# Taking the matrix values out of the gathers: an equality count on VectorE, and a scratch write among the row gathers

## The chip, the cores and the metric

The kernel runs on one core of one Trainium2 chip. A core has five engines that work side by side: PE (TensorE, matmul; its weight loads are listed apart as PEld), DVE (VectorE), ACT (ScalarE), POOL (GpSimd) and SP (SyncE, which here only issues transfers). Each takes its instructions in order and waits on semaphores for the others. The metric is the device time of one execution in microseconds, as the median of several runs without a profile.

## The reference, cut to what matters

Two graph layers run over one sparse matrix `adj` of 2708 x 2708 (about 1 % of it is not zero, and each row is divided by its number of entries, so all entries of a row are equal). Features are 128 wide.

```python
def layer0(X, A, W):                      # hyperbolic convolution
    XW = mobius_matvec(W, X)
    gamma = 2 / max(1 - sum(XW * XW), EPS)
    nominator   = A @ (gamma * XW)        # the dense product over adj
    denominator = clamp(A @ (gamma - 1))
    m = mobius_scalar_mul(0.5, nominator / denominator)
    return expmap0(relu(logmap0(mobius_scalar_mul(A.sum(-1), m))))

def layer1(x, A, msg_w, msg_b, upd_w, upd_b, ln_w, ln_b):
    s = x @ msg_w[:, :D].T
    d = x @ msg_w[:, D:].T
    messages   = gelu(s[:, None] + d[None, :] + msg_b)
    aggregated = einsum('ijd,ij->id', messages, A)      # only where A is not zero
    h = gelu(concat([x, aggregated]) @ upd_w.T + upd_b) + x
    return layernorm(h) * ln_w + ln_b

x = layernorm(x + layer0(x, adj, W))
x = layernorm(x + layer1(x, adj, ...))
```

## The kernel before

Rows are worked in 22 blocks of 128. While the dense product of layer 0 runs over a block of `adj`, the kernel also finds where the block is not zero: it takes signs, packs them into keys by matmul, reads the largest keys with `max`, and turns them into edges. The edges of a block are laid in tiles of 128, 99 tiles in all. For each tile it keeps `J` (the neighbour of each edge), `rid` (the edge's row within the block), `R` (a 0/1 matrix that carries rows to edges) and, before the change, `V` (the edge's value). GpSimd gathers V from the matrix in DRAM. Layer 1 then goes tile by tile: gather the neighbours' rows from a table, add, gelu, and sum by a matmul with `rv`.

```python
def gather(o, src, at):                                          # L189
    nc.gpsimd.indirect_dma_start(out=o, out_offset=None, in_=src,
        in_offset=bass.IndirectOffsetOnAxis(ap=at, axis=0))      # L191

def layer0(b):                                                   # one block
    aT = stream.tile([P, NB, P], F32, name="aT")                 # 2 buffers
    nc.sync.dma_start(aT, adj_t[b])                              # L317
    sgn = stream.tile([P, NB, P], BF16, name="sgn", bufs=1)
    nc.scalar.activation(sgn, aT, AF.Sign, accum_out=signs[:, b : b + 1])   # L319
    for j in range(NB):                                          # L324: the dense product
        if j in BREAKS: yield                                    # the steps of older blocks go in here
        nc.tensor.matmul(op[:, : D + 2], lhsT=aT[:, j, :], rhs=y[:, j, :], ...)
    nc.vector.scalar_tensor_tensor(nom[:, b, :], y[:, b, :], dg[:, b : b + 1], op, ...)   # L328
    ...                                                          # L332 ACT, L334 DVE: sums of squares

def keys(l, sgn):
    ...                                                          # L344, L350: keys by matmul into kp
    nc.vector.max(top[:, c : c + 8], seg[:, s, :])               # L358

def extract(l):
    ...                            # L378 to L389: lead, rest, second keys, m (in the list or not)
    nc.tensor.matmul(op[:, 0:2], lhsT=tri, rhs=db[:, 1:3], ...)  # L397, L398: running counts
    nc.scalar.copy(oe[:, l, :], op[:, 0:2])                      # L399
    nc.vector.scalar_tensor_tensor(mid, ...)                     # L402
    ...                            # L409 ACT, L412/L414 DVE: R from iota and mid
    yield
    ...                            # L419 to L429: bits, low, scan, code, z
    nc.tensor.matmul(sp[:, k, :], lhsT=R[:, t0 + k0 + k, :], rhs=z, ...)     # L438
    ...                            # L441, L446: nearest place; L444 rid
    nc.vector.scalar_tensor_tensor(J[:, t], near, -1.0, limit[:, t], ...)    # L447
    nc.vector.scalar_tensor_tensor(F[:, k0:k1], J[:, t], float(b * P * N - 1), rid[:, t], ...)  # L448
    for t in range(t0, t0 + n):
        gather(V[:, t : t + 1], adj.rearrange("i (j o) -> (i j) o", o=1), F[:, ...])

# between the layers
gd = nom
for g, n in quads:
    nc.scalar.activation(gd[:, g : g + n, :D], gd[:, g : g + n, :D], AF.Gelu)              # L583
    for k in range(n):
        nc.scalar.mul(gd[:, g + k, :D], gd[:, g + k, :D], dg[:, g + k : g + k + 1])        # L585

def messages(b, ag, tiles, ...):                                 # quads of up to four tiles
    for k, t in enumerate(ts):
        gather(dd[:, k, :], table..., J[:, t : t + 1])           # 7 quads of dd form a ring
        nc.tensor.matmul(X[:, k, :], lhsT=R[:, t, :], rhs=s_nm[:, b, :], ...)              # L652
        nc.vector.tensor_scalar(rv[:, k, :], iotaN, rid[:, t : t + 1], V[:, t : t + 1],
                                op0=OP.is_equal, op1=OP.mult)                              # L654
    nc.vector.tensor_tensor(dd, X, dd, op=OP.add)                # L657
    nc.scalar.activation(dd, dd, AF.Gelu)                        # L658
    for k in range(w):
        nc.tensor.matmul(ag[:, :P], lhsT=dd[:, k, :], rhs=rv[:, k, :], ...)                # L660

nc.scalar.copy(gd[:, b, :D], ag[:, :P])                          # L691, early blocks
nc.scalar.copy(agT, ag[:, :P])                                   # L702, all blocks
```

A dense fallback follows, taken only when a check on the lists fails; it does not run here.

## Time and profile before

| | |
|---|---|
| time, median of 3 runs | 389.42 us (389.2 to 390.23) |
| the profiled execution | 504.16 us, span 502.5 us, mean granted PE clock 0.783 |
| first product of layer 0 (L324) starts | 30.5 us into the span |
| last product of layer 0 starts | 268.3 us |
| first message sum (L660) starts | 344.6 us |
| last row gather starts | 451.75 us |
| GpSimd gathers of values | 99, median 944 ns each |
| GpSimd gathers of rows | 81 into `dd`, 18 into a free `aT` buffer, 944 ns each |
| transfers of `aT` | 22 of 1408 KB, median 6.7 us from issue to landing |

Times inside the span are those of one profiled execution, which is longer than the timed ones. In the lists of groups a line reads: source line, engine, operation, output and inputs with their sizes, count, then busy time, mean length in ns, and idle time of the engine before them with what ended it. In a timeline the first number is the start, the second the length. "remote" and "issue" mark waiting whose cause the trace does not show.

### The profile page before, as it was taken

The numbers are of one execution on the slowest core, as the hardware profiler recorded it, in microseconds if no ns is written. First come the engines' busy times: TensorE is split into PE (matmuls) and PEld (weight loads), VectorE is DVE, ScalarE is ACT, GpSimd is POOL, SyncE is SP. The second block draws the span as 40 slices with busy tenths as digits, with TensorE's granted clock in tenths as the row PEclk, the third lists the DMA queues.
The fourth block names the chain that finished last, engine by engine and source line by source line (L and its number), as shares of the span: only waits on it lengthen the run. The fifth ranks groups of instructions, "written<-read, shape, count | busy, mean of one in ns | idle before, by whom it ended". The sixth has DMA issues, their size and how long they took to land.

```text
span 502.5 us, 7784 instructions
## 1 busy us (share of the span) xinstructions
PE 333.5 (66%) x2427; PEld 297.2 (59%) x2427; DVE 275.9 (55%) x1474; ACT 208.0 (41%) x562; POOL 203.5 (40%) x297
## 2 busy tenths in 40 slices
PE   4269788674899989797973111538397697679620
PEld 4269677564889878795862001338395576557410
DVE  2979546433666565798740067248272226376671
ACT  2827325432657465794650022135032112326521
POOL 5301454571644525222257707722616572470000
PEclk9759779885999999998995555657679557798855
DMA  8306322223345544433421101110201120111100
GB/s 341 167 2 232 115 84 79 88 98 116 118 132 214 193 156 164 184 117 115 137 80 37 52 7 31 52 53 15 49 12 37 42 54 17 38 42 48 32 23 20
DMA packets 16237, 45.14 MB, mean 90 GB/s; under 512 B 5626, under 2 KB 11150, under 8 KB 13374
## 3 DMA queue, kind: packets, MB, share of 16 engines
q1 hardware_dynamic: 9710, 37.43, 20.6%
q0 software_dynamic: 6336, 6.55, 5.4%
q10 hardware_dynamic: 144, 0.60, 0.4%
q8 instruction: 20, 0.33, 0.3%
q14 instruction: 27, 0.22, 0.1%
HBM read 41.74 MB, written 2.83 MB: 89 GB/s over the span
## 4 chain that ended last, share of the span: by engine, by line
PE 32%; DVE 21%; issue 16%; another core or an unknown queue 14%; ACT 10%; DMA 4%; POOL 1%; DVEq 0%; POOLq 0%; ACTq 0%; SPq 0%
PE mp L324 7%; PE X L652 4%; PE mp L660 4%; PE kx L350 4%; PE sel L438 3%; DVE top L358 2%; ACT nom L635 2%; ACT sgn L319 2%; PE ag L660 2%; PE sel L612 1%; PE sel L613 1%; PE sel L610 1%; DMA xT<-in_x_t_dram 1%; DMA V<-in_adj_dram,F 1%
## 5 line engine op out<-in xcount | busy, mean ns | idle before, releaser
L191 POOL DMA_INDIRECT V<-in_adj_dram,F x99 | 94.9, 959 | 156.2 <-DVE top L358 31.0
L324 PE MATMUL mp<-y,aT 128*128 128x130 f32 x968 | 129.2, 288 | 1.4 <-DVE y L308 0.9
L324 PEld LDWEIGHTS mp<-y,aT 128*128 128x128 f32 x968 | 120.1, 199 | 2.3 <-DVE y L308 1.1
L191 POOL DMA_INDIRECT dd<-table_dram,J x81 | 78.1, 965 | 83.7 <-ACT agT L702 21.7
L319 ACT ACTIVATE sgn<-aT 128x2816 bf16<-128x2816 f32 x22 | 56.1, 2548 | 24.5 <-issue 20.5
L350 PE MATMUL kx<-kd,sgn 128*128 128x128 bf16 x484 | 41.5, 240 | 26.6 <-issue 19.1
L350 PEld LDWEIGHTS <-sgn 128*128 128x128 bf16 x484 | 33.3, 108 | 40.1 <-issue 31.4
L652 PE MATMUL X<-mx,R 128*128 128x128 f32 x198 | 41.1, 357 | 16.9 <-DVE dd L657 6.9
L654 DVE TENSOR_SCALAR rv<-iotaN,rid,V 128x128 f32<-128x128 f32 x99 | 30.1, 351 | 32.6 <-remote 20.0
L652 PEld LDWEIGHTS X<-mx,R 128*128 128x128 f32 x198 | 36.2, 265 | 19.2 <-DVE dd L657 7.5
L438 PE MATMUL sel<-z,R 128*128 128x49 f32 (+4 forms) x198 | 31.4, 299 | 23.3 <-DVE R L414 9.6
L438 PEld LDWEIGHTS sel<-z,R 128*128 128x128 f32 x198 | 28.3, 213 | 25.8 <-DVE R L414 10.4
L358 DVE MAX8 top<-kx 128x8 f32<-128x128 f32 (+3 forms) x152 | 28.6, 236 | 19.9 <-remote 14.8
L441 DVE TENSOR_TENSOR work<-sel,place 128x144 f32<-128x144 f32 (+11 forms) x29 | 11.7, 403 | 40.5 <-remote 30.9
L409 ACT ACTIVATE work<-iota,mid 128x512 f32<-128x512 f32 (+3 forms) x53 | 26.8, 553 | 5.5 <-DVE mid L402 5.4
L657 DVE TENSOR_TENSOR dd<-X,dd 128x384 f32<-128x384 f32 (+3 forms) x29 | 15.2, 526 | 21.7 <-remote 7.5
L444 ACT COPY rid<-sel 128x3 f32<-128x3 f32 (+5 forms) x29 | 4.7, 162 | 46.0 <-DVE work L441 36.3
L660 PE MATMUL mp<-rv,dd 128*128 128x128 f32 x116 | 21.6, 321 | 3.1 <-ACT dd L658 3.1
L402 DVE SCALAR_TENSOR_TENSOR mid<-sel,deg 128x2 f32<-128x2 f32 x25 | 3.9, 155 | 35.7 <-ACT oe L399 35.7
L610 PE MATMUL sel<-pk,xT 128*128 128x128 f32 x44 | 12.6, 377 | 16.4 <-ACT nom L614 10.4
L658 ACT ACTIVATE dd<-dd 128x384 f32<-128x384 f32 (+3 forms) x29 | 13.7, 497 | 20.3 <-DVE dd L657 14.5
L399 ACT COPY oe<-sel 128x2 f32<-128x2 f32 x25 | 4.0, 159 | 43.2 <-PE kx L350 25.9
(204 smaller groups left out, 614.6 us busy)
## 6 DMA issues: line engine op xcount, KB each, us to landing
aT<-in_adj_t_dram SPq DMA_DIRECT2D x22, 1408.0 KB, 6.7
V<-in_adj_dram,F POOLq DMA_INDIRECT x99
xT<-in_x_t_dram SPq DMA_DIRECT2D x2, 704.0 KB
x_sb<-in_x_nm_dram SPq DMA_DIRECT2D x2, 704.0 KB
out_dram<-nom SPq DMA_DIRECT2D x21, 64.0 KB, 1.6
dd<-table_dram,J POOLq DMA_INDIRECT x81
table_dram<-dt SPq DMA_DIRECT2D x5, 256.0 KB
pk<-in_pack_dram ACTq DMA_DIRECT2D x1, 587.5 KB
```

What stands on the lines that cost most here:

```text
L191: nc.gpsimd.indirect_dma_start(out=o, out_offset=None, in_=src, in_offset=bass.IndirectOffsetOnAxis(ap=at, axis=0))
L319: nc.scalar.activation(sgn, aT, AF.Sign, accum_out=signs[:, b : b + 1])
L324: nc.tensor.matmul(op[:, : D + 2], lhsT=aT[:, j, :], rhs=y[:, j, :], start=(j == 0), stop=(j == NB - 1))
L350: nc.tensor.matmul(kp[:, i * P : (i + 1) * P], lhsT=sgn[:, j, :], rhs=kd[:, q, :], start=False, stop=(i == len(groups) - 1 and j == j1 - 1),)
L358: nc.vector.max(top[:, c : c + 8], seg[:, s, :])
L409: nc.scalar.activation(r0, iota[:, k0 * P : k1 * P], AF.Abs, scale=2.0, bias=mid[:, k : k + 1])
L438: nc.tensor.matmul(sp[:, k, :], lhsT=R[:, t0 + k0 + k, :], rhs=z, start=True, stop=True)
L610: nc.tensor.matmul(up[:, :D], lhsT=x1T[:, s], rhs=wT[:, 2, :], start=True, stop=False)
L652: nc.tensor.matmul(X[:, k, :], lhsT=R[:, t, :], rhs=s_nm[:, b, :], start=True, stop=True)
L654: nc.vector.tensor_scalar(rv[:, k, :], iotaN, rid[:, t : t + 1], V[:, t : t + 1], op0=OP.is_equal, op1=OP.mult)
L657: nc.vector.tensor_tensor(dd, X, dd, op=OP.add)
L660: nc.tensor.matmul(ag[:, :P], lhsT=dd[:, k, :], rhs=rv[:, k, :], start=(first and k0 == 0 and k == 0), stop=(final and k0 + k == len(tiles ...
```

## The change

An edge's value is the same for the whole row of the matrix, and every row has its own diagonal element in it. So the value need not be fetched edge by edge: the sums can be made with ones, and multiplied at the end by the row's diagonal value. To be sure that this holds for the matrix at hand, VectorE compares every element of a block with the diagonal value of its row and counts the equal ones; the count is compared with the number of entries at the end, and the fallback is taken where they differ. So the gathers of V and the index F go; a 128 x 2816 comparison for each block comes, with a small load of the diagonal (`vb`); `rv` becomes a plain comparison for up to four tiles at once; the `dg` multiplications between the layers go; and the sum of a block is multiplied with a loaded row of diagonal values (`scaled`) where it was copied. Beside that the text has GpSimd write a scratch tile after each row gather, to keep two of them apart, and small column buffers are shared to make room.

```diff
@@ layer0
-    ss, ssp = cols(NB), cols(NB)
+    ss, ssp = (sc.tile([P, NB], F32, name=name) for name in ("ss", "ssp"))
     def layer0(b):
+        vb = stream.tile([P, P], F32, name="vb")
+        nc.sync.dma_start(vb, diag[:, b * P : (b + 1) * P].to_broadcast([P, P]))
         aT = stream.tile([P, NB, P], F32, name="aT")
         nc.sync.dma_start(aT, adj_t[b])
         sgn = stream.tile([P, NB, P], BF16, name="sgn", bufs=1)
         nc.scalar.activation(sgn, aT, AF.Sign, accum_out=signs[:, b : b + 1])
+        eq = stream.tile([P, NB, P], mybir.dt.uint8, name="eq", bufs=1)
+        nc.vector.scalar_tensor_tensor(
+            eq, aT, 1.0, vb.unsqueeze(1).to_broadcast([P, NB, P]),
+            op0=OP.mult, op1=OP.is_equal, accum_out=same[:, b : b + 1],
+        )
@@ extract
-        F = small.tile([P, TMAX], U32, name="F", bufs=3)
...
-            nc.vector.scalar_tensor_tensor(
-                F[:, k0:k1], J[:, t], float(b * P * N - 1), rid[:, t], op0=OP.add, op1=OP.add
-            )
-        for t in range(t0, t0 + n):
-            gather(V[:, t : t + 1], adj.rearrange("i (j o) -> (i j) o", o=1), F[:, t - t0 : t - t0 + 1])
@@ between the layers
         nc.scalar.activation(gd[:, g : g + n, :D], gd[:, g : g + n, :D], AF.Gelu)
-        for k in range(n):
-            nc.scalar.mul(gd[:, g + k, :D], gd[:, g + k, :D], dg[:, g + k : g + k + 1])
@@ messages
+    gap = edge.tile([P, P], F32, name="gap", bufs=1)
...
                 gather(dd[:, k, :], table[: SPLIT * P] if t in soon else table, J[:, t : t + 1])
+                nc.gpsimd.memset(gap, 0.0)
                 nc.tensor.matmul(X[:, k, :], lhsT=R[:, t, :], rhs=s_nm[:, b, :], start=True, stop=True)
-                nc.vector.tensor_scalar(
-                    rv[:, k, :], iotaN, rid[:, t : t + 1], V[:, t : t + 1], op0=OP.is_equal, op1=OP.mult
-                )
+            k = 0
+            while k < w:                      # runs of neighbouring tiles
+                n = next((i for i in range(1, w - k) if ts[k + i] != ts[k] + i), w - k)
+                nc.vector.tensor_tensor(
+                    rv[:, k : k + n, :], iotaN.unsqueeze(1).to_broadcast([P, n, P]),
+                    rid[:, ts[k] : ts[k] + n].unsqueeze(2).to_broadcast([P, n, P]), op=OP.is_equal,
+                )
+                k += n
@@ the sums of a block
+    def scaled(o, b, ag):
+        v = edge.tile([P, P], F32, name="v")
+        nc.scalar.dma_start(v, diag[:, b * P : (b + 1) * P].to_broadcast([P, P]))
+        nc.vector.tensor_mul(o, ag[:, :P], v)
...
-        nc.scalar.copy(gd[:, b, :D], ag[:, :P])
+        scaled(gd[:, b, :D], b, ag)
...
-            nc.scalar.copy(agT, ag[:, :P])
+            scaled(agT, b, ag)
@@ column buffers, the checks at the end and the host's layouts: cut
```

## The prediction

> **What bounds the kernel now.** I start with the span against the time. The profiled span is 502.5 us and the timed median is 389.42, so 113 us of what the trace shows belongs to the profiled execution. The trace tells where: added up over its records, there are 79 us in which PE, DVE and ACT all stand idle together, nearly all in pieces of 1 to 7 us that begin while GpSimd is in a run of gathers (111.1 to 118.1 and 270 to 291 are the plainest). Stretches without such pieces are what I price with. Then the busy totals, and the table by stretches:
>
> ```profile
> PE 333.5 (66%) x2427; PEld 297.2 (59%) x2427; DVE 275.9 (55%) x1474; ACT 208.0 (41%) x562; POOL 203.5 (40%) x297
> ```
>
> ```profile
> 30.50:57.00 26.50, 23.56 (x192) 22.09 (x192) 18.96 (x103) 12.21 (x33) 6.04 (x6) 0.89 0.31 110
> 133.00:173.00 40.00, 39.08 (x393) 36.79 (x391) 27.55 (x156) 26.87 (x64) 20.09 (x22) 1.00 0.52 182
> 208.00:232.00 24.00, 19.54 (x183) 18.56 (x180) 21.86 (x150) 19.77 (x51) 6.77 (x7) 1.00 0.45 165
> 338.00:452.00 114.00, 83.16 (x451) 73.33 (x452) 54.85 (x224) 31.62 (x91) 55.74 (x58) 0.72 0.13 34
> ```
>
> The columns are PE, PEld, DVE, ACT and POOL busy. From 133 to 173, the middle of the first layer, PE is busy for 39.08 of 40 us at full clock: PE bound. GpSimd, which gathers the values, has half its time over. From 208 to 232, when the first 16 blocks are also being finished, DVE is the fullest (21.86 of 24). After 338 nothing is full; there the row gathers set the pace. One middle block on PE, by time (start, length, instruction):
>
> ```profile
> 148.94 1.40 PE L350 MATMUL kx<-kd,sgn 128*128 128x128 bf16 x22
> 150.18 2.68 PE L324 MATMUL mp<-y,aT 128*128 128x130 f32 x22
> 152.69 1.00 PE L438 MATMUL sel<-z,R 128*128 128x57 f32 x8
> 153.53 1.79 PE L324 MATMUL mp<-y,aT 128*128 128x130 f32 x14
> 155.16 0.17 PE L397 MATMUL sel<-db,tri 128*128 128x2 bf16 x1
> 155.21 1.14 PE L324 MATMUL mp<-y,aT 128*128 128x130 f32 x8
> 156.60 1.40 PE L350 MATMUL kx<-kd,sgn 128*128 128x128 bf16 x22
> ```
>
> A block takes 156.60 - 148.94 = 7.66 us. From 165 on it takes 8.62, because L397 then waits for ACT; the mean of the middle blocks is about 8.1. DVE works 27.55 x 7.66/40 = 5.3 us of each block and idles the rest. The last views are the groups of instructions that the change touches, and ACT at the seam between the layers:
>
> ```profile
> L191 POOL DMA_INDIRECT V<-in_adj_dram,F x99 | 94.9, 959 | 156.2 <-DVE top L358 31.0
> L654 DVE TENSOR_SCALAR rv<-iotaN,rid,V 128x128 f32<-128x128 f32 x99 | 30.1, 351 | 32.6 <-remote 20.0
> L585 ACT ACTIVATE nom<-nom,pk 128x128 f32<-128x128 f32 x22 | 6.7, 392 | 0.0
> ```
>
> ```profile
> 334.50 1.15 ACT L583 ACTIVATE nom<-nom 128x512 f32<-128x512 f32 x2
> 335.55 2.44 ACT L585 ACTIVATE nom<-nom,pk 128x128 f32<-128x128 f32 x8
> ...
> 342.09 1.85 ACT L585 ACTIVATE nom<-nom,pk 128x128 f32<-128x128 f32 x6
> 343.84 2.38 ACT L658 ACTIVATE dd<-dd 128x512 f32<-128x512 f32 x5
> ```
>
> The first messages (L658) wait on ACT behind all the 22 multiplications of L585, though DVE had their input from 340.5 on.
>
> [...] In this trace the bars are 0.94 us with 0.30 between, so a gather occupies GpSimd for 1.25 us.
>
> **The change part by part.** *Removed: 99 value gathers.* 99 x 1.25 = 124 us of GpSimd, spread over a first layer in which GpSimd waits for the lists, not the reverse. The value V is first read at L654, after the layer. Worth near 0 on the path, with one exception: the last 9 of them stand among the row gathers (9 x 1.25 = 11 us), but row gathers past the ring's capacity wait for the first messages anyway. I count 0. The 29 instructions for F go too: 29 x 0.16 = 4.7 us of DVE.
>
> *Added: 22 compares of 128x2816 on DVE*, 22 x (3.09 + 0.08 for reading the sum) = 70 us, all in the first layer. What they cost depends on where they stand. In the order after the change a middle block has the compare right behind `mid`, ahead of R and z. That closes a loop between PE and DVE: L438 of one block (0.8 us), 14 matmuls (1.64), L397/L398 (0.2), ACT's oe and `mid` (0.6), one max (0.2), compare (3.1), then R, bits, scan, code, nom and z (2.5, their spacing between 155.79 and 157.94, with what the order now puts among them), and L438 of the next block. The sum is 9.05 us, against 5.9 without the compare. So the loop is longer than PE's 7.66 or 8.62 and sets the block.
>
> - Start: the compare of block 0 stands in the chain of small instructions that ends in y (18.4 to 30.5, without idle time): +3.1.
> - Blocks 1 to 7: DVE works 18.96 of 26.5 us at the start, and has 6 to 7 us a block later (35.4 us from 50 to 125, in which 5 to 6 blocks fall), because the lists are long. The loop is near 10.5 against 8.7 to 9: about 7 x 1.8 = +12.
> - Blocks 8 to 15: 8 x (9.05 - 8.1) = +7.5.
> - Blocks 16 to 21: DVE has 2 us over in 24, so a compare of 3.1 costs most of itself: 6 x 2.3 = +14.
>
> Together +36 us.
>
> *The seam.* L585 leaves: 22 x 0.305 (its spacing) = -6.7 us of ACT, straight on the path. I count -6, since DVE's own chain there is only a little shorter.
>
> *The messages.* L654 (99 x 0.351) becomes one compare for up to four tiles, about 0.6 us by the 128x512 instructions of L308 (639 ns): some 30 to 16 us. DVE has room there, so -2. Scaling moves from the input to the output: a DVE multiplication takes the place of an ACT copy (0.26), and 30 loads of a 64 KB row tile are issued from ACT, each of which waits for the multiplication two blocks back. In the fast stretch of the early messages that could add 0.4 us to each of 8: +3.
>
> *GpSimd's memsets.* The text puts one between two row gathers, but in the order after the change all 99 stand ahead of the first gather. At 0.2 us each (the memset of `ones`, 128x128, took 0.21) they end near 35 us, before anything needs GpSimd. The gathers remain 1.25 us apart. Cost 0.
>
> Sum: 36 - 6 - 2 + 3 = +31, or 420 us. The estimate of the loop leaves out that the scheduler can give something back where PE has a reserve, so I take 414.
>
> **The rivals.** *The value gathers hold the kernel up in the timed runs too.* For it: the common idle pieces begin in runs of gathers, and DVE waits 30.9 us for "remote" at L441. Against it: L441 waits only for PE's own matmuls, and the timed run is 113 us shorter than the span. With the common idle taken away (502.5 - 79 = 423) the trace is still longer than 389, which leaves no room for them. If the rival is right, 99 fewer gathers give back 20 to 40 us and the time is 370 to 395.
>
> *The compare hides.* DVE idles 2.4 us in a middle block. If the loop is looser than I think, only the start, the long lists and blocks 16 to 21 pay, at half my figures: +15 - 6 = about 398.
>
> *DVE becomes the bound everywhere,* at 5.3 + 3.1 - 0.2 us and all waits around it: 10 us a block, +55, or 438. For it: DVE takes its instructions in order, and a 3 us instruction in front delays R, on which PE waits.
>
> *GpSimd sets the end.* From the first table on it has 99 + 9 gathers, 135 us. If that chain is tight, the 11 us count: 403.
>
> **Range and chances.** The certain parts are the compare's length and its number; the uncertain one is how much of 70 us falls on the path: I take half. A quarter gives 400, three quarters 437. The range is 388 to 434. Faster needs the first rival at full size: 0.10. Within 2% (381.6 to 397.2) needs the compare mostly hidden: 0.13. Slower: 0.77.
>
> **What would show it.** In the profile after: 22 compares of about 3.1 us; DVE fuller than PE through the first layer; a block period near 9 us with L438 waiting for DVE's z; PE's share lower; the first L658 no longer behind L585; POOL with 99 gathers, and the memsets in one row near 16 to 35 us. I am wrong if PE is still full in the middle of the layer, if the first layer is shorter in the timed sense[...].

## The result and the profile after

The kernel after takes 440.01 us (median of 4 runs, 438.73 to 441.39), the kernel before 389.83 us beside it (4 runs). The ratio is 1.129, with a 95% interval of 1.124 to 1.133: the change costs 50 us. The prediction was 414 us, with a range up to 434.

First the page of the profile after (span 439.7 us): the engines' totals, then four of the costliest groups.

```profile
PE 312.2 (71%) x2427; PEld 282.7 (64%) x2427; DVE 322.9 (73%) x1459; ACT 198.7 (45%) x510; POOL 134.1 (30%) x297
...
L333 PE MATMUL mp<-y,aT 128*128 128x130 f32 x968 | 129.0, 293 | 16.3 <-DMA aT<-in_adj_t_dram 15.9
L325 DVE SCALAR_TENSOR_TENSOR eq<-aT,vb 128x2816 uint8<-128x2816 f32 x22 | 67.7, 3079 | 0.0
...
L663 DVE TENSOR_TENSOR rv<-iotaN,rid 128x384 f32<-128x384 f32 (+3 forms) x35 | 18.4, 529 | 4.9 <-PE mp L673 3.9
L657 POOL MEMSET gap<- 128x128 f32 x99 | 20.2, 204 | 5.6
```

The new compares last 3079 ns each. GpSimd's total falls from 203.5 to 134.1 us: the value gathers are gone, 99 memsets of 204 ns are there. The new entry is the last field of L333: the dense product now waits 15.9 us for `aT`, the block of the matrix. In the profile of the kernel before that line waited 1.4 us in all, and not for `aT`:

```profile
L324 PE MATMUL mp<-y,aT 128*128 128x130 f32 x968 | 129.2, 288 | 1.4 <-DVE y L308 0.9
```

The view of waits of the kernel after shows both halves of PE waiting (us in total, times, longest):

```profile
PEld mp L333 <- DMA aT<-in_adj_t_dram: 21.4, 12, 3.8
...
PE mp L333 <- DMA aT<-in_adj_t_dram: 15.9, 10, 3.7
...
PEld sel L446 <- DVE z L438: 2.7, 2, 2.1
```

The third line is the wait that the prediction expected to govern, PE's weight loads waiting for DVE's `z` (L438 before is L446 after): 2.7 us in all.

Now the kernel after by stages. They are cut at events of the program, so that other kernels can be cut alike: the first dense product; the end of block 7's product (its `nom`); that of block 15; the first row gather; the last gelu of the messages. Columns are busy PE, PEld, DVE, ACT and POOL, then PE's granted clock.

```profile
33.80:116.00 82.20, 73.55 (x646) 69.14 (x646) 69.60 (x274) 45.12 (x106) 6.99 (x35) 0.93 0.38 129
116.00:186.00 70.00, 62.71 (x605) 59.19 (x605) 58.19 (x245) 40.92 (x95) 0.00 (x0) 0.98 0.51 174
186.00:263.50 77.50, 53.02 (x414) 47.47 (x412) 60.94 (x303) 38.83 (x100) 0.00 (x0) 0.85 0.33 111
263.50:407.00 143.50, 105.51 (x677) 92.83 (x676) 96.25 (x434) 46.67 (x121) 101.08 (x99) 0.81 0.26 66
```

Two readings matter. Up to block 15 neither engine is full: PE has 8.65 and 7.29 us over, DVE 12.6 and 11.8. In the third stage (blocks 16 to 21 and the chain of small instructions that ends layer 0) nothing is full either, and PE falls to 53 of 77.5 us. Its longest wait there is for `R`:

```profile
234.79 1.46 PE L446 MATMUL sel<-z,R 128*128 128x49 f32 x4 [9.39 <-DVE R L423]
```

On DVE that `R` stands behind a compare (from 224.83) and, from 227.84 to 234.34 us, behind the small instructions of the layernorm that ends layer 0 for the first 16 blocks.

What lies between two blocks shows in PE by time, around two middle blocks:

```profile
142.09 3.18 PE L333 MATMUL mp<-y,aT 128*128 128x130 f32 x26 [1.77 <-DMA aT<-in_adj_t_dram]
145.11 0.99 PE L446 MATMUL sel<-z,R 128*128 128x57 f32 x8
...
149.79 3.18 PE L333 MATMUL mp<-y,aT 128*128 128x130 f32 x26
152.80 1.01 PE L446 MATMUL sel<-z,R 128*128 128x49 f32 x8
...
159.35 0.82 PE L333 MATMUL mp<-y,aT 128*128 128x130 f32 x5 [1.78 <-DMA aT<-in_adj_t_dram]
```

One block lasts 149.79 - 142.09 = 7.70 us, the next 9.56: every second block waits for `aT`. The DMA issues on SyncE's queue (start, length) and DVE's part of the same block say what `aT` waits for:

```profile
133.43 0.33 SPq L318 DMA_DIRECT2D vb<-in_diag_dram  x1
133.86 0.37 SPq L320 DMA_DIRECT2D aT<-in_adj_t_dram  x1
...
150.71 0.33 SPq L318 DMA_DIRECT2D vb<-in_diag_dram  x1
151.14 0.37 SPq L320 DMA_DIRECT2D aT<-in_adj_t_dram  x1
```

```profile
147.32 0.16 DVE L411 SCALAR_TENSOR_TENSOR mid<-sel,deg 128x2 f32<-128x2 f32 x1
...
147.60 3.07 DVE L325 SCALAR_TENSOR_TENSOR eq<-aT,vb 128x2816 uint8<-128x2816 f32 x1
...
152.45 0.21 DVE L438 SCALAR_TENSOR_TENSOR z<-scan,code 128x48 f32<-128x48 f32 x1
```

`aT` has two buffers. A buffer is free when the last reader of its block has ended, and since the change that is the compare: it ended at 133.40, the row load `vb` was issued at 133.43, `aT` only at 133.86, behind it on the same queue, and PE's product started on it at 142.09, 8.2 us later. The block's own compare began 5.5 us after that (147.60) and ended at 150.67; then came the next `vb` (150.71) and the next `aT` (151.14). So the loop through one buffer lasts 151.14 - 133.86 = 17.3 us, and as there are two buffers, it allows one block every 8.6 us. That is what the blocks take on the mean here: (7.70 + 9.56) / 2 = 8.6. In the second excerpt, compare, R and `z` follow each other without idle time; from the compare's start to the end of `z` it is 5.06 us.

Last the seam between the layers, ACT by time:

```profile
301.62 0.37 ACT L536 COPY dt<-X 128x256 f32<-128x256 f32 x1 [2.78 <-DMA table_dram<-dt]
...
307.53 0.63 ACT L671 ACTIVATE dd<-dd 128x512 f32<-128x512 f32 x1 [2.62 <-DVE dd L670]
```

From the last copy of the table to the first gelu of a message: 5.9 us, and ACT waits for DVE in it, no longer for its own work.

### The profile page after: what moved, and what is told of

The parts are those of the page before. It is cut to its first block, busy times and chain, and to the rows that moved or that the text cites. A ratio compares the mean times of both kernels' runs of the same rounds, so it can differ in the third digit from the quotient of the medians.

```text
span 439.7 us, 7750 instructions
## 1 busy us (share of the span) xinstructions
PE 312.2 (71%) x2427; PEld 282.7 (64%) x2427; DVE 322.9 (73%) x1459; ACT 198.7 (45%) x510; POOL 134.1 (30%) x297
## 4 chain that ended last, share of the span: by engine, by line
PE 29%; DVE 27%; DMA 26%; ACT 7%; issue 5%; POOL 3%; SPq 0%; POOLq 0%; ACTq 0%; DVEq 0%
DMA aT<-in_adj_t_dram 17%; PE mp L333 13%; DVE eq L325 6%; DMA dd<-table_dram,J 4%; PE sel L446 3%; POOL dd L192 3%; ACT sgn L322 2%; DMA table_dram<-dt 2%; PE mp L673 2%; PE X L658 2%; DMA v<-in_diag_dram 2%; PE kx L359 1%; DVE top L367 1%; PE X L532 1%; DMA xT<-in_x_t_dram 1%
## 5 line engine op out<-in xcount | busy, mean ns | idle before, releaser
L192 POOL DMA_INDIRECT dd<-table_dram,J x81 | 82.6, 1019 | 245.2 <-DVE top L367 220.8
L333 PE MATMUL mp<-y,aT 128*128 128x130 f32 x968 | 129.0, 293 | 16.3 <-DMA aT<-in_adj_t_dram 15.9
L333 PEld LDWEIGHTS mp<-y,aT 128*128 128x128 f32 x968 | 121.7, 204 | 23.4 <-DMA aT<-in_adj_t_dram 21.4
L325 DVE SCALAR_TENSOR_TENSOR eq<-aT,vb 128x2816 uint8<-128x2816 f32 x22 | 67.7, 3079 | 0.0
L359 PE MATMUL kx<-kd,sgn 128*128 128x128 bf16 x484 | 35.2, 227 | 10.3 <-ACT sgn L322 10.3
L658 PE MATMUL X<-mx,R 128*128 128x128 f32 x198 | 32.1, 295 | 11.9 <-DVE dd L670 9.8
L446 PE MATMUL sel<-z,R 128*128 128x49 f32 (+4 forms) x198 | 29.7, 288 | 14.3 <-DVE R L423 10.3
L446 PEld LDWEIGHTS sel<-z,R 128*128 128x128 f32 x198 | 26.7, 203 | 16.0 <-DVE R L423 11.0
L658 PEld LDWEIGHTS X<-mx,R 128*128 128x128 f32 x198 | 27.1, 202 | 14.4 <-DVE dd L670 11.1
L663 DVE TENSOR_TENSOR rv<-iotaN,rid 128x384 f32<-128x384 f32 (+3 forms) x35 | 18.4, 529 | 4.9 <-PE mp L673 3.9
L657 POOL MEMSET gap<- 128x128 f32 x99 | 20.2, 204 | 5.6
L673 PEld LDWEIGHTS mp<-rv,dd 128*128 128x128 f32 x116 | 19.6, 246 | 2.4 <-ACT dd L671 1.4
L192 POOL DMA_INDIRECT aT<-table_dram,J x18 | 18.5, 1029 | 5.5 <-issue 4.6
L617 ACT ACTIVATE nom<-sel 128x128 f32<-128x128 f32 x22 | 6.0, 273 | 30.2 <-PE sel L616 29.0
```

What stands on the lines that cost most here:

```text
L325: nc.vector.scalar_tensor_tensor(eq, aT, 1.0, vb.unsqueeze(1).to_broadcast([P, NB, P]), op0=OP.mult, op1=OP.is_equal, accum_out=same[:, b ...
L359: nc.tensor.matmul(kp[:, i * P : (i + 1) * P], lhsT=sgn[:, j, :], rhs=kd[:, q, :], start=False, stop=(i == len(groups) - 1 and j == j1 - 1),)
L657: nc.gpsimd.memset(gap, 0.0)
L663: nc.vector.tensor_tensor(rv[:, k : k + n, :], iotaN.unsqueeze(1).to_broadcast([P, n, P]), rid[:, ts[k] : ts[k] + n].unsqueeze(2).to_broad ...
```

## The experiments

The theory after the result was that the loss sits in the compare, and that it has several causes which the totals don't separate: DVE's time, the order of DVE's other instructions, the buffer of `aT` held for longer, and the row load in front of `aT`. The rival was that the messages' half (sums with ones, multiplication at the end, loads of `v`) lost what the compare did not. A third account, from the prediction, was that the value gathers held the kernel before up.

In most of what follows, ratios are to the kernel before on the same chip, with 95% intervals. They are needed: beside these experiments the kernel before took 388.7 to 390.2 us on three of five chips and about 500 us on the two others, and only the first kind can be set against 440 us. Experiments 5 to 8, 17 and 18 ran on the second kind.

**1. The kernel before without value gathers.**

```diff
+    nc.gpsimd.memset(V, 1.0)
-        for t in range(t0, t0 + n):
-            gather(V[:, t : t + 1], adj.rearrange(...), F[:, t - t0 : t - t0 + 1])
```

It leaves out the values, so that it sums over a matrix of ones. The index `F` is still computed, and the order of PE, ACT and DVE stays that of the kernel before.

> The kernel before without its 99 value gathers (V filled once with 1.0, so the sums are those of a matrix of ones; everything else and the order of the other instructions as before). Theory of the prediction: the gathers cost nothing in a timed run, and are what stretches the profiled one: 387 to 391 us, and the profiled span falls from 502 us to within 5 us of the time. Rival: the gathers hold the timed run up too: 370 to 380.

Measured: 379.93 us, ratio 0.976 (0.971 to 0.981): by the ratio 9.4 us less, by the medians (388.7 before) 8.8. The gathers were not free, as the prediction had it, nor worth 20 to 40 us.

**2 to 4. The compare taken apart, order held.** In these three every engine keeps the order of instructions that it has in the kernel after, by ordering edges between successive instructions, so that nothing moves but what is named. The number of equal elements is taken from the row counts instead. Number 2 has no compare and no row loads; number 3 has a compare of the same length in the same place that reads only constants; number 4 compares `aT` with ones.

```diff
 # 2
-        vb = ...; nc.sync.dma_start(vb, ...)
-        nc.vector.scalar_tensor_tensor(eq, aT, 1.0, vb..., accum_out=same[:, b : b + 1])
 # 3: vb and its load gone, and
+            eq, pk[:, :P].unsqueeze(1).to_broadcast([P, NB, P]), 1.0, ones.unsqueeze(1)...,
 # 4: vb and its load gone, and
+            eq, aT, 1.0, ones.unsqueeze(1).to_broadcast([P, NB, P]),
```

> The changed kernel without the 22 comparisons and their row loads, every engine's order held as in the changed kernel. If the comparison is the whole of the loss, this is 383 to 390 us (the time before less the seam's 6, plus the loads' 3). If the messages' half of the change costs more than the 3 us predicted, it stays above 395.

> The changed kernel with each comparison made of the same length at the same place of VectorE's order, but on constants: it neither reads aT nor vb, and the row loads are left out; orders held. Theory 1 (VectorE's time in front of R and z is the cost): as the changed kernel, 432 to 440. Theory 2 (the comparison keeps the aT buffer 2.5 us longer, and the load of the block after next waits for it): near the run without comparisons, at most 400.

> The changed kernel with the comparison reading aT as it does, but against a constant, so that the 22 row loads (64 KB each) ahead of the aT loads are gone; orders held. Theory 3 (the row loads lengthen the aT loads, 8.1 us to landing against 6.7 before, and this lies in the loop of the two aT buffers): 420 to 430. Theories 1 and 2: 436 to 441.

Measured: number 2, 410.63 us, ratio 1.056 (1.050 to 1.061); number 3, 418.34 us, 1.075 (1.069 to 1.080); number 4, 425.34 us, 1.093 (1.087 to 1.098). So DVE's time is worth 8 us of 70, reading `aT` (which holds its buffer for longer) 7 us, the row loads 15 us. Number 3 fell between both of its expected ranges. The surprise is number 2: without any compare, the kernel still takes 410.6 us. By what was expected of it, a time above 395 us would mean that the messages' half is what costs; number 10 shows that it isn't.

**5 and 10. No compare, order chosen anew.** As number 2, but the scheduler may order the instructions as it likes. Number 5 ran on a chip of the second kind, number 10 on one of the first.

```diff
-        vb = ...; nc.sync.dma_start(vb, ...)
-        nc.vector.scalar_tensor_tensor(eq, aT, 1.0, vb..., accum_out=same[:, b : b + 1])
```

> The same kernel without comparisons and row loads as in the earlier run (410.6 us), but the scheduler orders the engines anew, as it does for a kernel that never had a comparison. In the held run the chain of small VectorE instructions that ends layer 0 of the first 16 blocks took 28 us where the kernel before without value gathers needs 18, because it stands behind matmuls that VectorE waits for. Theory 4 (the order that the comparison brought about costs this): the first row gather falls from 235 to some 215 us and the time to 386 to 392. Rival (the small buffers, of which the change keeps one copy where there were two, cause it): 402 to 411 still.

> No comparison, engines ordered anew, once more. On a chip like the first: 212 us to the first row gather (as on the second chip) and some 174 from there to the end, so 384 to 388; that would put 22 to 26 of the 50 us down to the order that came with the comparison. On a chip like the second: 459 to 463.

Measured: number 10, 387.53 us in 20 runs, ratio 0.992 (0.990 to 0.995). Number 5, 461.0 us where the kernel before took 500.67, ratio 0.929 (0.920 to 0.938). The stages of number 10, cut as above:

```profile
31.40:99.00 67.60, 67.44 (x614) 63.81 (x614) 54.37 (x280) 42.32 (x108) 9.13 (x44) 0.96 0.42 151
99.00:160.00 61.00, 61.00 (x616) 57.88 (x616) 41.41 (x235) 41.99 (x100) 0.00 (x0) 1.00 0.53 191
160.00:213.10 53.10, 49.73 (x442) 45.37 (x443) 45.35 (x278) 38.16 (x96) 0.01 (x1) 0.97 0.45 157
213.10:354.50 141.40, 104.17 (x680) 91.09 (x677) 94.59 (x432) 46.56 (x120) 97.39 (x99) 0.82 0.28 67
```

PE is full through two stages: 67.44 of 67.60 and 61.00 of 61.00. Against the profile after, the stages are shorter by 14.6, 9.0, 24.4 and 2.1 us. So the compare's part is 52 us, and nearly all of it lies before the first row gather; the rival that blames the messages falls. And 410.6 - 387.5 = 23 us of it is not the compare's time but the order that the scheduler chose around it. The other small change, column buffers that are shared, is in number 10 too, so it can't be what costs the 52 us by itself. The profiles by stages, in us, cut at the ends of the same events (so they differ by up to 0.4 us from the windows above):

| kernel | start | blocks to 7 | 8 to 15 | 16 to 21 and the end of layer 0 | messages and end | span |
|---|---|---|---|---|---|---|
| 10: no compare, free order | 31.4 | 67.8 | 60.8 | 53.0 | 173.9 | 387.0 |
| 2: the order of after | 32.1 | 74.9 | 60.1 | 68.4 | 173.8 | 409.2 |
| 3: and DVE's time | 33.5 | 76.1 | 61.3 | 71.2 | 174.4 | 416.6 |
| 4: and reading `aT` | 33.6 | 76.2 | 61.3 | 74.7 | 177.8 | 423.6 |
| after: and the row loads | 33.8 | 82.6 | 69.7 | 77.5 | 176.2 | 439.7 |

The order costs in the first blocks and most of all in the third stage. The row loads cost in blocks 0 to 15, where the wait for `aT` is. Reading `aT` costs nothing there; half of its 7 us is in the third stage and half among the messages, where no compare runs any more, and that half isn't explained. These parts hold for adding one thing after the other in this sequence.

In number 2 the chain that ends layer 0 stands on DVE behind instructions that wait for PE. DVE of number 2, by time, shows one place (its line numbers are shifted):

```profile
175.23 0.17 DVE L341 TENSOR_SCALAR c<-c 128x16 int32<-128x16 int32 x1
...
178.49 0.31 DVE L557 TENSOR_TENSOR work<-sel,place 128x144 f32<-128x144 f32 x1 [3.00 <-PE sel L554]
...
178.72 0.17 DVE L343 TENSOR_TENSOR c<-c 128x16 f32<-128x16 f32 x1
179.08 0.17 DVE L344 SCALAR_TENSOR_TENSOR c<-c,c 128x16 f32<-128x16 f32 x1
```

The instructions on `c` are steps of that chain, each 0.17 us. The next step waits 3 us behind `work`, which waits for matmuls of a later block. From the end of block 15's `nom` to the first ReLU, which needs the chain's result, it is 32.3 us in number 2, 17.6 in number 1 and 17.5 in number 10. In the kernel after it is 39.0: of the 24.4 us that its third stage has over number 10's, 21.5 lie in this chain.

**6. The compare alone.** The compare and row loads of the kernel after, with the messages, sums and copies of the kernel before; V is all ones and not gathered.

```diff
+    nc.gpsimd.memset(V, 1.0)
-            nc.vector.tensor_tensor(rv[:, k : k + n, :], ..., op=OP.is_equal)
+                nc.vector.tensor_scalar(rv[:, k, :], iotaN, rid[...], V[...], op0=OP.is_equal, op1=OP.mult)
-        scaled(gd[:, b, :D], b, ag)
+        nc.scalar.copy(gd[:, b, :D], ag[:, :P])
```

> The comparison and the row loads alone: messages, rv, the seam's 22 multiplications and the copies as in the kernel before, V filled once with 1.0 and no value gathers (the sums are those of a matrix of ones). If the loss lies in the first layer and the messages' half is nearly free: first row gather at 258 to 268 us, time 430 to 438. If the messages' half (the loads of v, the multiplications at the end) costs 7 to 10 us as the spans of the two halves suggest, then 428 to 432; if the comparison is only what the first runs took away with it (30 us), 405 to 412.

Measured, on a chip of the second kind: 513.35 us, ratio 1.035 (1.023 to 1.047). What can be carried over is the time of the first row gather, which without value gathers is nearly the same on both kinds of chip (212.45 us in number 5, 213.1 in number 10): 264.8 us, against 263.5 in the profile after. The whole loss up to there comes with compare and row loads alone.

**7 and 11. The memsets really between the gathers.** In the kernel after all 99 memsets run ahead of the first row gather. Here each stands behind its gather in GpSimd's order, and the other engines' orders are held.

```diff
 # GpSimd's order
-  memset memset memset ... gather gather gather
+  gather memset gather memset gather memset ...
```

> The changed kernel with each of GpSimd's 99 writes of the scratch tile really behind its gather; all other orders held. If the row gathers, back to back at 1.25 us, set the end from the first of them on, 99 writes of 0.2 us add 15 to 20 us: 455 to 460. If the messages are held by PE and VectorE instead: 440 to 445. If a write hides in the 0.30 us between two gathers: 439 to 443, and the spacing stays 1.25 us.

> GpSimd's writes really between the gathers. On the second chip the gathers stood 1.34 us apart with them, 1.25 without, so on a chip like the first 99 x 0.09 = 9 us if GpSimd sets the pace from the first row gather on: 446 to 450 against the changed kernel's 440. On a chip like the second the writes could pay, by breaking the runs: 8 us or more under the changed kernel of this call.

Measured: number 11, 446.05 us, ratio 1.138 (1.129 to 1.147), 6.4 us above the kernel after on the same chip (439.66, experiment 9); the runs of the two overlap (439.9 to 447.7 against 437.6 to 442.5), so the 6.4 is rough. Number 7, on the second kind: 503.5 us, ratio 1.011 (0.996 to 1.026). GpSimd of number 11 by time:

```profile
270.88 0.95 POOL L300 DMA_INDIRECT dd<-table_dram,J  x1 [0.17 <-issue]
271.83 0.22 POOL L765 MEMSET gap<- 128x128 f32 x1
272.22 0.95 POOL L300 DMA_INDIRECT dd<-table_dram,J  x1 [0.17 <-DVE c L579]
```

Gathers are 1.34 us apart, against 1.25 without the memset between: 99 x 0.09 = 9 us of GpSimd, some 6 of them on the path. From the first row gather to the last it is 137.6 us, against 128.3 in number 9. So the memset's stated purpose costs something and brings nothing on this chip; its accidental place ahead of all gathers costs nothing.

**8 and 12. No loads of `v`.** The multiplication uses ones, so that the last factor is missing; order held.

```diff
-        nc.vector.tensor_mul(o, ag[:, :P], v)
+        nc.vector.tensor_mul(o, ag[:, :P], ones)
```

> The changed kernel without the 30 loads of v: the sums are multiplied with a resident tile of ones (so the output lacks the last factor), orders held. The prediction's 3 us for the loads: 436 to 438. If ScalarE's waiting for v is what makes the last part longer (3 to 5 us from the last row gather to the end): 434 to 436. If nothing waits for them: 439 to 441.

> No loads of v (sums multiplied by ones, so the output lacks the last factor). On a chip like the first: 436 to 438 by the prediction's 3 us, 433 to 436 if the waits for v are what makes the stretch from the first row gather to the end 10 us longer than in the kernel before without value gathers (176 against 166), 439 to 441 if nothing waits for them. On a chip like the second: no claim beyond the same difference to the changed kernel of this call.

Measured: number 12, 441.33 us, beside 439.66 of the kernel after. Three of its four runs took 441.1 to 442.1 us and one 432.3, so the times alone aren't sharp; but from the last row gather to the end its profile has 47.4 us, those of the kernel after 46.2 and 47.5 (number 9). The loads cost nothing that can be seen. Number 8 took 511.36 us on the second kind, where the kernel after was not run, and says nothing on this. It can be set beside number 7, though, which has the loads and its memsets between the gathers: 503.5 us, and the longest run of number 7 (506.0) is shorter than the shortest of number 8 (506.7). So on such a chip the write between gathers may give back some 8 us; that the loads of `v` are free there too was not shown.

**9. The kernel after again**, for the chip of numbers 10 to 12.

> The changed kernel itself, as the reference of this call, because the four runs of the call before were on a chip on which the kernel before takes 500 us and its runs of gathers leave the other engines idle. If this chip is like the first: 438 to 441 against 389. If it is like the second: the change should lose less, since it has no value gathers that could stop the first layer: 495 to 515 against 500.

Measured: 439.66 us, ratio 1.127 (1.120 to 1.134).

**13. An order made by hand.** All of the work of the kernel after, with the order of number 10; each compare is put in front of the DVE instruction that waits longest for PE within its block, and `vb` is loaded behind `aT`.

```diff
 # DVE's order in a middle block
-  ... mid  eq  R  bits  scan  code  z ... work
+  ... mid  R  bits  scan  code  z ... eq  work
```

> All the work of the changed kernel, comparisons and row loads too, but in another order: every engine as in the run without comparisons (387.5 us), each comparison put into VectorE's order just ahead of the instruction that waits longest for PE in its block (1.37 us idle there), and each row load behind its aT load. If the 50 us are mostly order, buffer and queue (theories 2, 3, 4) and VectorE's 8.5 us a block set the rest: 405 to 416. If the comparison costs its length wherever it stands: 430 to 440.

Measured: 426.57 us, ratio 1.089 (1.084 to 1.094). That misses both expected ranges, and is no better than number 15. Its stages are 86, 69, 63.9 and 143.3 us: the third gains 13.6 us on the kernel after, and the blocks to 7 lose 3.8 on it, perhaps because the buffer is released later when the compare stands later; that wasn't tried apart. So the 23 us of order can't simply be had back by returning to the order of number 10: with the compares in it, the blocks to 7 take 18 us more than there.

**14. Comparing only in the last blocks.** The kernel before, in which blocks 19 to 21 (6 tiles) take V from the diagonal by a small matmul with R, and only those blocks are compared, behind their product. The other blocks keep their value gathers.

```diff
+            if b >= OWN:      # 19
+                nc.tensor.matmul(vp[:, k, :], lhsT=R[:, t0 + k0 + k, :], rhs=dg[:, b - 1 : b + 1], ...)
+                nc.scalar.copy(V[:, t], vp[:, :, 1])
-        for t in range(t0, t0 + n):
+        for t in range(t0, t0 + n if b < OWN else t0):
             gather(V[:, t : t + 1], ...)
```

> A version from what was found: the kernel before, which keeps its value gathers for blocks 0 to 18, where GpSimd is idle; only the last three blocks (6 tiles), whose value gathers stood among the row gathers, take the row's diagonal value through a small matmul with R, and are checked by a comparison each, behind their product. 6 gathers of 1.25 us less in the chain of row gathers: 381 to 385. If the value gathers' 9 us came from something else than those last ones: 387 to 391. If three comparisons at that place cost the first layer as much as they save: 388 to 394.

Measured: 390.33 us in 22 runs, ratio 0.999 (0.997 to 1.002). The first row gather starts at 208, but the last table copy is at 262.6 us instead of 250.3 in number 1: what the gathers gave at one end is lost at the other, and no net gain is left: a miss of the 381 to 385 us hoped for.

**15. The row load behind `aT`.** The kernel after with two lines moved, order free.

```diff
-        vb = stream.tile([P, P], F32, name="vb")
-        nc.sync.dma_start(vb, diag[...])
         aT = stream.tile([P, NB, P], F32, name="aT")
         nc.sync.dma_start(aT, adj_t[b])
+        vb = stream.tile([P, P], F32, name="vb")
+        nc.sync.dma_start(vb, diag[...])
```

> The changed kernel with one line moved: the row load of a block is issued behind its aT load, not ahead of it; engines ordered anew by the scheduler. If the 15 to 18 us between the changed kernel and the one without row loads come from aT landing 2 us later behind them: 422 to 430. If they come from the bytes or from the scheduler's luck: 436 to 442.

Measured: 424.33 us, ratio 1.085 (1.080 to 1.089): 15.7 us less than the kernel after, for the same work. The scheduler moved other instructions too (some 75 of DVE's 1459), but number 4, with the order held and no row loads at all, saves as much, in the same stages. Number 15's stages up to the first row gather, then two of its waits and two of its DMA issues:

```profile
33.50:110.00 76.50, 70.48 (x650) 66.05 (x650) 69.63 (x275) 45.25 (x106) 7.05 (x35) 0.97 0.40 141
110.00:172.00 62.00, 61.40 (x608) 57.80 (x607) 57.80 (x244) 42.81 (x96) 0.00 (x0) 1.00 0.55 196
172.00:248.30 76.30, 53.35 (x409) 46.89 (x408) 61.22 (x304) 38.90 (x98) 0.04 (x1) 0.85 0.33 112
```

```profile
PEld mp L333 <- DMA aT<-in_adj_t_dram: 7.7, 7, 3.3
...
PE mp L333 <- DMA aT<-in_adj_t_dram: 4.7, 5, 3.2
```

```profile
aT<-in_adj_t_dram SPq DMA_DIRECT2D x22, 1408.0 KB, 5.9
...
vb<-in_diag_dram SPq DMA_DIRECT2D x22, 64.0 KB, 5.8
```

The same view of DMA issues in the kernel after:

```profile
aT<-in_adj_t_dram SPq DMA_DIRECT2D x22, 1408.0 KB, 8.1
...
vb<-in_diag_dram SPq DMA_DIRECT2D x22, 64.0 KB, 4.3
```

Here a load of 64 KB ahead of one of 1408 KB delays the large one's landing from 5.9 to 8.1 us after its issue (6.2 in number 10, which has no row loads), and its issue by 0.4. PE's waits for `aT` fall from 15.9 to 4.7 us, and in the middle stage PE is at 61.40 of 62.00 with the compare in it: there the compare hides.

**16. ScalarE copies the sums.** Number 10 with an ACT copy in place of DVE's multiplication and without `v`; the last factor is missing.

```diff
-        nc.vector.tensor_mul(o, ag[:, :P], v)
+        nc.scalar.copy(o, ag[:, :P])
```

> No comparisons (387.5 us), and the finished sums copied by ScalarE as in the kernel before, not multiplied by VectorE (so the output lacks the last factor; no loads of v). The kernel before without value gathers takes 380. If the multiplication in VectorE's queue, behind additions that wait for gathered rows, makes that difference: 379 to 382. If the multi-tile rv does: 386 to 388.

Measured: 391.88 us in 6 runs (386.8 to 394.6), ratio 1.005 (1.001 to 1.010), not faster than number 10 (0.992), and outside both expected ranges. The multiplication on DVE isn't what the messages' half pays for.

**17. The end of layer 0 first.** Number 15 with the steps of the chain that ends layer 0 for blocks 0 to 15 put at high priority, so that the scheduler places them early.

```diff
+            with tc.high_priority():
                 for e in ends:
                     next(e, None)
```

> The changed kernel with the row loads behind (424 us) and, beside that, the steps that end layer 0 of the first 16 blocks traced at high priority, so that the scheduler puts that chain of small VectorE instructions ahead. From the product of block 15 to the first row gather the kernel without comparisons takes 53 us, the one with row loads behind 76, of which the comparisons themselves are 4 x 3.1 = 12. If the chain's place in the order is the rest: 412 to 418. If the scheduler's order there is as good as the comparisons allow: 422 to 426.

Measured, on the second kind of chip: 488.2 us where the kernel before takes 499.34, ratio 0.976 (0.963 to 0.988). It can't be set against the expected times, which are for the first kind. Its first row gather is at 240.7 us, against 248.3 in number 15, with block 15 ended within 1 us of it (171 and 172): about 7 us of the order's cost can be had back. Experiment 15 is at 424.3 us on the other kind, so that 7 us would not bring it to 389 there; that sum is an estimate, it wasn't run.

**18. The kernel before itself**, on the same chip as number 17, with a profile.

> The kernel before, as it was, for a profile from a chip on which it takes 389 us: the profile that the prediction was made from shows 502. If the 79 us of common idle time are that one chip's: total idle time of 10 to 20 us, and the first layer as without value gathers. Where the value gathers cost the 9 us: if among the last blocks' row gathers, the first row gather starts near 213 and the last one near 347 (338 without them); if they slow the first layer itself, the first row gather is late by those 9 us.

Measured: 497.39 us (2 runs), and a profiled span of 499.5 us, with stage times near those of the first profile of before (first row gather at 256.2 and 255.0 us). The profile from a chip on which the kernel takes 389 us was not had.

## Why the prediction was right or wrong

**The sum.** The prediction counted +36 for the compare, -6 for the seam, -2 and +3 for the messages and 0 for the gathers, and then took 6 off. Scaled to 390 us, the runs give -9.4 for the gathers (1), +6.4 for the seam and the messages' half (10 against 1), +36 for the compare with its row load behind `aT` (15 against 10) and +17 for having the row load ahead (after against 15): 390 - 9 + 6 + 36 + 17 = 440. The direction was right. The step that failed is "Added: 22 compares of 128x2816 on DVE". It priced DVE's 3.1 us by a loop between PE and DVE through `z`, and gave the small load `vb` nothing, though the diff puts it in front of `aT` on the same queue. The runs show another loop in its place, through the two buffers of `aT`: in the kernel after PE waits 2.7 us for `z` and 15.9 us for `aT`, and putting the load behind gives back 15.7 us. That term alone carries the time from 423 out of the predicted range. In all the compare and its load cost 52 us where the step counted 36.

**The +36 by its parts.** Without the load in front, the compare costs 36 to 38 us (15 against 10), so that the 36 looks right; that is luck, for the parts are not, and the kernel that was predicted has the load in front. Both against number 10, stage by stage:

| part | predicted, us | number 15, us | the kernel after, us |
|---|---|---|---|
| start | 3.1 | 2.1 | 2.4 |
| blocks to 7 | 12 | 8.9 | 14.6 |
| blocks 8 to 15 | 7.5 | 1.0 | 9.0 |
| blocks 16 to 21 and the end of layer 0 | 14 | 23.2 | 24.4 |
| messages and end | - | 2.5 | 2.3 |

- *The loop in the middle blocks* was to take 9.05 us, "longer than PE's 7.66 or 8.62". Measured from the profile after: compare start to the end of `z` 5.06 us, and compare to compare 155.31 - 147.60 = 7.71 us. The chain inside a block was there as drawn; two terms were too long, the 14 matmuls behind L438 (8 stand there) and R to `z` (2.0 instead of 2.5 us). At 7.7 us it is as long as PE's own block, so the compare hides, as number 15 shows (61.40 of 62.00 us). That was the second rival, and it holds for this stage only. The kernel after does have blocks near 9 us, 70.0 / 8 = 8.75 on the mean, but for another reason, the wait for `aT` in every second one. So 9.0 us measured beside 7.5 predicted is no success: the number nearly agrees and the wait is the wrong one. The view of waits tells the two apart.
- *The base of 8.1 us a block* came from the long profile; without a compare, number 10 needs 61.0 / 8 = 7.6.
- *Blocks 16 to 21* were priced from DVE's idle time, 2 us in 24. The measured loss there is larger, and comes mostly with the order: 15.4 of the 24.4 us are there without any compare (2 against 10). The prediction looked at where the scheduler put the compare and not at what the compare moved: the chain of small instructions behind waits for PE. It even took 6 us off because "the scheduler can give something back"; the order that it chose costs 23 (2 against 10).
- *The range.* "Three quarters" of the compares' 70 us on the path is what happened (52), and the prediction itself put that at 437, and its third rival at 438. Both lay outside its own range, which ended at 434.

**The seam.** The reason was right: L585 is gone from ACT, and the stretch from the last table copy to the first gelu shrank from 9.6 us in number 1 to 5.9. It gained nothing that the total shows, because ACT doesn't set the pace there: the row gathers do. In the profile after they run from 263.5 to 394 us, from 269.1 on without a pause of more than half a microsecond, 1.25 us apart at the median.

**The messages.** `rv` went as expected (35 instructions, 18.4 us in place of 30.1), with DVE not the limit. The loads of `v` cost nothing (12). Still the half costs about 6.4 us net of the seam. It lies at the far end: from the last row gather to the end of the program it is 41.6 us in number 1 (337.6 to 379.2) and 47.6 in number 10 (339.4 to 387.0). It isn't the multiplication (16) and not the loads (12). Whether the wider `rv`, the shared column buffers or the order of the last messages against the update steps does it wasn't tried apart, and stays open.

**The gathers.** "Worth near 0", with the 11 us of the last nine considered and dismissed as the fourth rival, was wrong: number 1 gains 9.4 us. The size is close to the 11 us of nine gathers among the row gathers. Number 14 speaks for them: with 90 of the value gathers ahead of it, its first row gather is at 208.3 us, no later than the 212.8 of number 1 without any, so those 90 don't hold the first layer up. That it was the nine is still only argued; no profile of the kernel before on a chip of the first kind exists to show the nine, and number 14, which takes only the last six tiles' gathers away, gained nothing net. (The matrix is thinner than the text above the prediction says: 99 tiles of 128 hold at most 12672 edges, and with the diagonal that is 0.2 % of it, not 1 %.)

**The 113 us between span and time.** The prediction put it down to "the profiled execution". The runs speak against it: on the chip of number 18 a run of the kernel before without a profile takes 493.6 us too, and on the first kind a profiled run is as long as the others (kernel after: 441.4, others 438.7 to 440.2). So the profile of before most likely came from a chip of the second kind, and its 113 us belong to that chip and not to the profiling. The first rival leaned on the idle pieces in that profile; on the timed chips it is 9.4 us, not 20 to 40. Where the time is 500 us, the rival has more for it: number 5, without value gathers and compare, is 7% faster there, and number 17, with the compare, 2.4% (1.2 to 3.7).

**What was to show it.** Right: 22 compares of 3.1 us (3079 ns at the median, 3072 to 3089, and 82 ns more for reading the sum: 22 x 3.16 = 69.5 us, where 70 was said), 99 gathers, memsets in one row (at 16.2 to 42.8 us, where 16 to 35 was said), the first gelu of the messages free of L585. Wrong: DVE is fuller than PE only in blocks 16 to 21 (60.94 against 53.02), not through the whole layer, and `z` is not what PE waits for. PE's share (66% before, 71% after) says nothing, since the two profiles are of the two kinds of chip. The profile of before has no compare and no DVE instruction longer than 1.23 us, so the 3.09 us was not shown there. An estimate from its trace comes near it: L618 (TENSOR_TENSOR) takes 418 ns for 128x256 and 1227 ns for 128x1024, so 1.05 ns for each further element, and 1.227 + 1792 x 0.00105 = 3.11 us for 128x2816. Compare and memsets cost each other nothing that the trace shows: the compare at 20.68 us, beside the row of memsets, lasted 3.08 us as the others did, and all 99 memsets took 200 to 226 ns.

## What to carry to other kernels

A small load put ahead of a large one in a double-buffered loop can be paid by whoever waits for the large one (16 of 440 us here): look at what the queue issues between the buffer's release and the load that matters, and put the small load behind. A long instruction on an engine that has time over can cost much more than its own time (here 52 us, of which its time was 8), because it may become the last reader of a buffer (reading `aT` cost 7 us) and because the scheduler arranges other chains around it (the order cost 23 us). Price both, and take the instruction away once with the order held and once with the order free. A profile whose span differs by a quarter from the timed runs (502.5 us against 389.4 here) may be from another chip: make sure of the chip before its idle pieces are explained.

## What the runs showed of the hardware

The kernel before takes 388.7 to 390.2 us on three chips and 499 to 501 on two. The long executions have stretches in which PE, DVE and ACT all stand idle while GpSimd gathers: 70 to 81 us in all in profiles 5, 6, 8, 17 and 18, and 11 to 17 us in profiles on the other chips. The plainest is in number 5. GpSimd issues 41 gathers in an unbroken run, from 212.45 to 263.69 us; two windows of that profile:

```profile
215.00:240.00 25.00, 6.04 (x57) 4.83 (x56) 3.47 (x23) 3.63 (x12) 18.93 (x20) 0.70 0.21 53
240.00:270.00 30.00, 0.00 (x0) 0.00 (x0) 0.00 (x0) 0.00 (x0) 17.96 (x19) 0.50 0.18 44
```

and DVE of the same profile by time:

```profile
229.50 0.19 DVE L466 RECIPROCAL c<-c 128x6 f32<-128x6 f32 x1
270.18 0.30 DVE L360 MAX8 top<-kx 128x8 f32<-128x128 f32 x1 [40.49 <-remote]
```

Between 229.7 and 270.2 us no other compute engine runs an instruction. Number 10 is the same kernel on a chip of the first kind, and in its windows the other engines work on beside the gathers:

```profile
215.00:240.00 25.00, 8.61 (x72) 7.45 (x71) 19.26 (x138) 10.09 (x31) 18.91 (x21) 0.70 0.20 54
240.00:270.00 30.00, 22.14 (x137) 19.29 (x138) 23.59 (x84) 9.27 (x19) 22.99 (x24) 0.79 0.27 70
```

DVE is busy for 23.59 of the 30 us there, against none. A write between the gathers may have been meant for this; with the memsets between them (7) the idle total is still 56.5 us, though in pieces of at most 6.1 us, against up to 12.1 in number 8, whose memsets run ahead, and 40.5 in number 5. What stops the engines, and why on these chips alone, stays open: the restart at 270.18 comes 6.5 us after the run of gathers ends, and the trace names no cause for it ("remote", 40.49 us). The 44 GB/s of the second window of number 5 are about what 20 gathers of 64 KB move in 30 us, so by that estimate the transfers there are the gathers' own.
